# Attention plus feed-forward block: row exponentials of the first 128-row block gathered into one instruction, the sigmoid by exp and log, and small pieces evicted one unit later

## The chip, the cores and the metric

The kernel runs on one core of one Trainium2 chip. The metric is the device time of one execution in microseconds (us). A core has TensorE (PE; its weight loads are a row of their own, PEld), VectorE (DVE), ScalarE (ACT), GpSimd (POOL) and SyncE (SP, which here only issues DMAs). Each engine works through its own instructions in order and waits on semaphores for the others. Matmuls write to PSUM, eight banks of 128 partitions x 512 fp32; the other data lie in SBUF.

## The reference, cut to what matters

The input is 16 batches of 512 rows of 128 numbers. With `xn` the layer-normalised input, the output is `x + attention(xn) + ffn(xn)`:

```python
# attention: 16 heads, q and k of width 8, v of width 64, causal
scores = q @ k.T / sqrt(8); attn = softmax(scores masked above the diagonal); ctx = attn @ v; out = ctx @ Wo
# ffn: x_prev is xn one row earlier (zero at the first row)
xr = mu_r * xn + (1 - mu_r) * x_prev
xk = mu_k * xn + (1 - mu_k) * x_prev
r = sigmoid(xr @ W_r.T)
out = r * ((relu(xk @ W_k.T) ** 2) @ W_v.T)
```

## The kernel before, in words

All line numbers are those of the kernel before. A batch `b` is cut into 4 groups `g` of four heads (two pairs `w`, two heads `u` in each pair), and a group into 5 units `t`. So a batch has 20 units, and a unit number `n` runs through all batches (`n0 = 20 b`; in what follows "unit 14" is unit `n0 + 14`). `unit_work` (line 530) issues one unit. It does work for three places at once:

- For the group that is 11 units ahead, `rowscores` and `rowmask` (330, 343) compute on PE a 128-row block of scores for four heads, `sm`, two PSUM banks at a time with two buffers (`ps_sm`, 92); `rowmax` (357) takes the negated row maxima `negm` on DVE. `ROWS` (303) says which row blocks `i` a unit holds: kinds 0 and 2 a block of 384 columns (`i` = 2) and one of 128 (`i` = 0) for one pair; kinds 1 and 3 the 512 columns of `i` = 3; kind 4 the 256 columns of `i` = 1 for both pairs.
- For the group 10 units ahead (`LEAD`, 26), `rowsum` (376) does, for every block and head, one exp on ACT with the row's maximum as bias and the row sum as a second result (`accum_out`). After kind 4, `log_sums` (387) takes the logs; one unit later `sub_logs` and `turn_stats` (392, 396) turn `negm - log z` into rows by a PE transpose, `pm`, and `put_stats` (407) writes these, two units later, into extra rows of `q` by four DMAs on POOL's queue.
- For the unit itself, `scores` (422) computes the transposed scores `sT` (one buffer of two banks, `ps_st`, 93) with the softmax's normalisation already inside, `weights` (433) does one 128x1024 exp on ACT into `e` and zeroes the part above the diagonal on POOL, and `weigh` (445) multiplies by `v` into `av` (one bank, `ps_av`, 94), which `take_ctx` (460) copies out on DVE at the head of kinds 0 and 2.

Every other product goes through one PSUM bank, `m` (`ps_m`, line 95, one buffer): v (`project_v`, 245, eight per batch), q and k (`project_qk`, 218, each evicted twice, as a rounded high part `qh` and the remainder `ql`), the transposed input (`transpose_xn`, 207), the ffn products `ffn_r`, `ffn_k`, `ffn_out` (265, 284, 292), the output projection (`project_out`, 466, eight accumulating parts in two halves), and `pm`. I call these pieces.

The order is written out by hand. All engines keep the order in which the program issues instructions (`_InOrder`, 34). A table `at(n, piece)` (490 to 528) says in which unit a piece is issued; within a unit the order is: row scores, transposed scores, mask, `sub_logs`, `take_ctx`, `rowmax`, `rowsum`, `weights`, the pieces with their evictions, `weigh` (in kind 1 `weigh` comes ahead of the pieces), `turn_stats`. A piece's eviction is thus behind the unit's `rowmax` on DVE. Before, q is projected in unit 12, k in unit 17, v in units 1, 5, 10, 13, 14, 15, 16 and 18, the other ffn pieces in 0, 11 and 19, the transposes in 6, and the output projection of the batch before in 2, 2, 3, 4, 7, 7, 8, 9.

```python
def weights(b, g, t):
    e = ep.tile([P, 2, 512], FP, tag="e", name=f"e_{b}_{g}_{t}")
    act.activation(e, sts.pop((b, g, t)), AF.Exp)
...
def m_tile(name):
...
    return ps_m.tile([P, 512], FP, tag="m", name=name)
```

Of the kernel before, what the change touches and what calls it, by code (L numbers as in the profile page):

```python
# [27 lines left out]


FAR, NEAR = 2.0**43, 2.0**-84  # L30
SIG_MIN = -87.5


class _InOrder:
# [15 lines left out]
def attn_ffn_kernel(  # L50
# [156 lines left out]
    def transpose_xn(b):  # L207
        xn = xs.pop((b, "n"))
        pt = m_tile(f"xnTp_{b}")
        for c in range(NB):  # L210
            pe.transpose(pt[:, c * P : (c + 1) * P], xn[:, c, :], ident)

        xnT = big.tile([P, T + 1], FP, tag="xnT", name=f"xnT_{b}")
        pool.memset(xnT[:, 0:1], 0.0)
        dve.tensor_copy(xnT[:, 1 : T + 1], pt)
        xnTs[b] = xnT

    def project_qk(b, is_k, queue=sp):

        w, name = (wk, "k") if is_k else (wq, "q")  # L220
        pq = m_tile(f"p{name}_{b}")
        product(pq, w, xnTs[b][:, 1 : T + 1])
        hi = one.tile([P, T], FR, tag=f"{name}h", name=f"{name}h_{b}")
        lo = one.tile([P, T], FR, tag=f"{name}l", name=f"{name}l_{b}")
        dve.tensor_copy(hi, pq)
        dve.tensor_tensor(lo, pq, hi.bitcast(FP), ALU.subtract)

        blocks = (hi, lo, hi) if is_k else (hi, lo)
        d = dram.tile([len(blocks), P, T], FP, tag=name, name=f"{name}_{b}")
        for n, half in enumerate(blocks):  # L230
            queue.dma_start(out=d[n], in_=half.bitcast(FP))
        halves[b, name] = d.rearrange("n (d p u) t -> u (n d) p t", u=2, d=DK)
# [12 lines left out]
    def project_v(b, j, i):  # L245
        if j == 0 and i == 0:
            vs[b] = big.tile([P, NB, H * DV], FP, tag="v", name=f"v_{b}")
        pv = m_tile(f"pv_{b}_{j}_{i}")
        product(pv, xnTs[b][:, 1 + j * P : 1 + (j + 1) * P], wv[:, i * 512 : (i + 1) * 512])
        dve.tensor_copy(vs[b][:, j, i * 512 : (i + 1) * 512], pv)  # L250

    def mix_prev(b, i):
        prev = one.tile([P, T], FP, tag="prev", name=f"prev_{b}_{i}")
# [11 lines left out]
    def ffn_r(b):  # L265
        pr = m_tile(f"pr_{b}")
        product_turned(pr, xmix.pop((b, 0)), ffn_w[:, 0, :])
        e = one.tile([P, T], FP, tag="e_sig", name=f"e_sig_{b}")

        dve.tensor_scalar(e, pr, SIG_MIN, None, ALU.max)  # L270
        ffns[b, "e"] = e

    def ffn_exp(b):
        e = ffns[b, "e"]
        act.activation(e, e, AF.Exp, scale=-1.0)
        pool.tensor_scalar(e, e, 1.0, None, ALU.add)

    def ffn_sig(b, c):
        if c == 0:
            ffns[b] = one.tile([P, T], FP, tag="sig", name=f"sig_{b}")  # L280
        cols = slice(c * P, (c + 1) * P)
        dve.reciprocal(ffns[b][:, cols], ffns[b, "e"][:, cols])

    def ffn_k(b):
        pk = m_tile(f"pk_{b}")
        product(pk, ffn_w[:, 1, :], xmix.pop((b, 1)))
        kr = one.tile([P, T], FP, tag="kr", name=f"kr_{b}")
        dve.tensor_scalar(kr, pk, 0.0, None, ALU.max)
        pool.tensor_tensor(kr, kr, kr, ALU.mult)
        ffns[b, "k"] = kr  # L290

    def ffn_out(b):
        pk = m_tile(f"pkv_{b}")
        product_turned(pk, ffns.pop((b, "k")), ffn_w[:, 2, :])
        f = small.tile([P, T], FP, tag="ffn", name=f"ffn_{b}")
        dve.tensor_tensor(f, pk, ffns[b], ALU.mult)

        pool.tensor_tensor(f, f, xs.pop(b).rearrange("p c d -> p (c d)"), ALU.add)
        ffns[b] = f

# [22 lines left out]
        return (b, g, t) if 0 <= b < B else None  # L325


    stats, sms = {}, {}

    def rowscores(b, g, t):  # L330
        q, k = qs[b % 2], ks[b % 2]
# [25 lines left out]
    def rowmax(b, g, t):  # L357
# [11 lines left out]
            )  # L369
            return  # L370
        for w, i, to in blocks:
            dve.tensor_reduce(
                negm[:, :, w, i], sm[:, :, to : to + (i + 1) * P], AX.X, ALU.max, negate=True
            )

    def rowsum(b, g, t):
        negm, z = stats[b, g]
        sm = sms.pop((b, g, t))
        for w, i, to in ROWS[t]:
            for u in range(2):  # L380
                cols = sm[:, u, to : to + (i + 1) * P]
                act.activation(
                    cols, cols, AF.Exp,
                    bias=negm[:, u, w, i : i + 1], accum_out=z[:, u, w, i : i + 1],
                )

    def log_sums(b, g):
        lz = stat.tile([P, 2, 2, NB], FP, tag="lz", name=f"lz_{b}_{g}")
# [77 lines left out]
    def project_out(b, p):  # L466

        half = NPAIR // 2
        if p % half == 0:
            ffns[b, "po"] = m_tile(f"po_{b}_{p}")  # L470
        po = ffns[b, "po"]
        product_turned(
            po, ctxs.pop((b, p)), wo[:, p, :], start=(p % half == 0), stop=(p % half == half - 1)
        )
        if p == half - 1:
            y = one.tile([P, T], FP, tag="y", name=f"y_{b}")
            dve.tensor_tensor(y, po, ffns[b], ALU.add)
            ffns[b] = y
        elif p == NPAIR - 1:
            o = small.tile([P, NB, D], FP, tag="o", name=f"o_{b}")  # L480
            dve.tensor_tensor(o.rearrange("p c d -> p (c d)"), po, ffns.pop(b), ALU.add)
            sp.dma_start(out=out[b].rearrange("(c p) d -> p c d", p=P), in_=o)

    todo, subs, turns, puts = {}, {}, {}, {}

    def at(n, f, *args):  # L490
        todo.setdefault(n, []).append((f, args))

    per = UNITS * NPAIR // 2
    for b in range(B):
        n0 = b * per
        if b + 1 < B:
            r = 0 if b else 7
            at(n0 + r, ffn_r, b + 1)  # L500
            at(n0 + r + 1, ffn_exp, b + 1)
            for m, n in enumerate((1 if b else 3, 5, 10, 13, 14, 15, 16, 18)):
                at(n0 + n, project_v, b + 1, m // 2, m % 2)
            at(n0 + 6, mix_prev, b + 1, 1)
            at(n0 + 8, mix, b + 1, 1)
            at(n0 + 11, ffn_k, b + 1)
            at(n0 + 19, ffn_out, b + 1)
            for m, n in enumerate((-1, -1, 0, 0, 4, 4, 5, 5) if b else (0, 0, 0, 0, 4, 4, 5, 5)):
                at(n0 + n, spread_qk, b + 1, *SPREAD[m], slice(0, NPAIR // 2))
            for m, n in enumerate((8, 9, 9, 10, 10, 14, 14, 15)):  # L510
                at(n0 + n, spread_qk, b + 1, *SPREAD[m], slice(NPAIR // 2, NPAIR))
        if b + 2 < B:
            at(n0 + 4, deviation, b + 2)
            for c in range(NB):
                at(n0 + (1, 1, 3, 3)[c], row_moments, b + 2, c)
                at(n0 + 4 + c // 2, normalise, b + 2, c)
            at(n0 + 6, transpose_xn, b + 2)
            at(n0 + 12, project_qk, b + 2, False)
            at(n0 + 17, project_qk, b + 2, True)
            at(n0 + 11, mix_prev, b + 2, 0)  # L520
            at(n0 + 13, mix, b + 2, 0)
        for p, n in enumerate((2, 2, 3, 4, 7, 7, 8, 9) if b < B - 1 else (-8, -7, -7, -6, -3, -2, 0, 3)):
            at(n0 + per + n, project_out, b, p)
        if b + 1 < B:
            for c, n in enumerate((3, 7, 9, 14) if b else (11, 14, 17, 18)):
                at(n0 + n, ffn_sig, b + 1, c)
        if b + 3 < B:
            at(n0 + 11, load_x, b + 3)

    def unit_work(n):  # L530
# [10 lines left out]
        if n in subs:  # L541
            sub_logs(*subs.pop(n))
        t = n % UNITS
        done = {0: (n - UNITS, 0), 2: (n - UNITS, 1)}.get(t)
        if done and unit_of(done[0]):
            b, g, _ = unit_of(done[0])
            take_ctx(b, 2 * g + done[1])
        if stat_next:
            rowmax(*stat_next)

        if stat_now:
            rowsum(*stat_now)
            b, g, kind = stat_now
            if kind == UNITS - 1:
                log_sums(b, g)
                subs[n + 1] = turns[n + 1] = puts[n + 2] = b, g
        if now:
            weights(*now)
        pieces = todo.pop(n, ())
        if t != 1:  # L560
            for f, args in pieces:
                f(*args)
        since, w, blocks = WEIGHED[t]
        if unit_of(n - since):
            b, g, _ = unit_of(n - since)
            for j in blocks:
                weigh(b, 2 * g + w, j, (t, j) in ((1, 3), (4, 3)))
        if t == 1:
            for f, args in pieces:
                f(*args)  # L570
        if n in turns:
            turn_stats(*turns.pop(n))

    halves = {}

    qs, ks = [], []
# [18 lines left out]
    deviation(0)  # L595
    for c in range(NB):
        normalise(0, c, dve)
    transpose_xn(0)
    project_qk(0, False)
    project_qk(0, True, act)  # L600

# [36 lines left out]
    deviation(1)  # L640
    for c in range(NB):
        normalise(1, c, dve)
    transpose_xn(1)
    project_qk(1, False)
    first = -LEAD
    at(first + 1, project_qk, 1, True)
    for m, part in enumerate(SPREAD):
# [4 lines left out]
        at(first - 1 + 5 * i, mix_prev, 0, i)  # L652
        at(first + 1 + 6 * i, mix, 0, i)
    at(first + 8, ffn_r, 0)
    at(first + 9, ffn_exp, 0)
    for c, n in enumerate((1, 2, 3, 3)):
        at(n, ffn_sig, 0, c)
    at(2, ffn_k, 0)
    at(4, ffn_out, 0)
    at(1, mix_prev, 1, 0)  # L660
    at(5, mix, 1, 0)
    for n in range(first - 1, B * per + 2):
        if n == -1:
            lent.clear()
# [1 line left out]
    take_ctx(B - 1, NPAIR - 1)  # L666
    for n in sorted(todo):
        for f, args in todo[n]:
            f(*args)


# [29 lines left out]
```

## Time and profile before

| what | value |
|---|---|
| median of 3 runs | 1014.96 us (1014.45 to 1015.54) |
| the profiled execution, its own time | 1015.34 us |
| its span, first to last instruction | 1013.6 us |
| mean granted TensorE clock | 0.975 (1.00 in every stretch from 100 to 943 us) |
| logs `lz` of four successive groups, start | 508.03, 522.58, 537.12, 552.28; the next 567.36 us |
| one batch (20 units), from these | 59.33 us |
| first and last 128x1024 exp `e` (start) | 58.39 and 1002.38 us |

Nearly all instructions carry line 44, since a helper records them; they are told apart by their tiles. A group line gives out<-in by the program's names, the shapes, the count, then busy time in us and mean ns of one instruction, then the idle time of the engine just before and what ended it. A fp32 matmul appears as two records, so "x4" of `pv` is two products. A timeline line has start, length, engine, operation and, in brackets, idle time before it with its releaser. Instructions of one engine overlap at their ends, so I count a step from its start to the start of the next, not by its own length.

### The profile page before, as it was taken

What the parts mean: (1) busy time and instruction counts of PE and PEld (TensorE: products, weight loads), DVE (VectorE), ACT (ScalarE), POOL (GpSimd) and SP (SyncE); (2) the same over time, 40 slices, a digit from 0 to 9 for tenths busy, and PEclk for the clock granted to TensorE, in tenths of its full rate; (3) what the DMA queues carried; (4) which work ended last, traced back from release to release, by engine and by line L of the source; (5) the groups of instructions that cost most, each with busy time, mean ns of one, the idle gap of its engine ahead of it and who ended that gap; (6) DMA issues with size and microseconds to landing.
All of it is one profiled execution on the core that took longest, in us unless ns stands there. A gap on an engine that the chain in (4) does not pass through costs nothing.

```text
span 1013.6 us, 22825 instructions
## 1 busy us (share of the span) xinstructions
PE 949.4 (94%) x8131; PEld 524.4 (52%) x8131; DVE 790.4 (78%) x1312; ACT 921.6 (91%) x2449; POOL 512.4 (51%) x959
## 2 busy tenths in 40 slices
PE   3888999999999999999999999999999999999997
PEld 1244464555546455554645555464555646455454
DVE  4777878787887878788787878878787887877641
ACT  0688999999999999999999999999999999999982
POOL 4146364554646455454645555464465546434431
PEclk8578999999999999999999999999999999999999
DMA  8730513535142353514235341423534131343000
GB/s 183 134 45 13 110 19 70 91 70 91 34 101 28 70 91 70 90 34 99 31 70 90 70 91 34 96 34 70 90 71 81 33 95 25 70 80 49 3 13 11
DMA packets 59968, 67.10 MB, mean 66 GB/s; under 512 B 12928, under 2 KB 33024, under 8 KB 59856
## 3 DMA queue, kind: packets, MB, share of 16 engines
q1 hardware_dynamic: 48688, 61.89, 32.4%
q10 hardware_dynamic: 2528, 2.43, 1.0%
q0 software_dynamic: 8640, 1.34, 1.0%
q8 instruction: 65, 1.06, 0.5%
q14 instruction: 47, 0.39, 0.1%
HBM read 39.13 MB, written 25.17 MB: 63 GB/s over the span
## 4 chain that ended last, share of the span: by engine, by line
ACT 55%; PE 27%; issue 8%; DVE 7%; DMA 2%; POOL 1%; ACTq 0%; POOLq 0%
ACT sm L44 37%; ACT e L44 17%; PE av L44 9%; PE po L44 5%; DVE negm L44 4%; PE sm L44 4%; PE pv L44 3%; PE sT L44 3%; PE xnTp L44 1%; PE pr L44 1%; DVE xnT L44 1%; DMA q<-ml 1%; DVE v L44 1%; DMA k<-k 1%; PE pk L44 1%
## 5 line engine op out<-in xcount | busy, mean ns | idle before, releaser
L44 ACT ACTIVATE sm<-sm,negm 128x384 f32<-128x384 f32 (+3 forms) x1024 | 513.0, 501 | 64.9 <-DMA k<-k 27.3
L44 DVE TENSOR_REDUCE negm<-sm 128x2 f32<-128x768 f32 (+3 forms) x448 | 397.9, 912 | 101.3 <-PE sm L44 99.2
L44 POOL TENSOR_SCALAR_AFFINE_SELECT e<-e 128x256 f32<-128x256 f32 x512 | 200.5, 410 | 432.4 <-ACT e L44 432.3
L44 PE MATMUL av<-e,v 128*64 128x512 f32 (+3 forms) x2048 | 336.5, 438 | 2.4 <-DVE ctx L44 2.4
L44 ACT ACTIVATE e<-sT 128x1024 f32<-128x1024 f32 x320 | 324.1, 1013 | 14.1 <-PE sT L44 14.1
L44 PEld LDWEIGHTS av<-e,v 128*64 128x64 f32 x2048 | 139.7, 137 | 161.6 <-issue 129.6
L44 ACT ACTIVATION_READ_ACCUMULATOR sm<-sm,negm 128x1 f32 x1024 | 200.5, 196 | 0.0
L44 PE MATMUL sm<-k,q 33*128 33x384 f32 (+3 forms) x1024 | 164.8, 378 | 7.4 <-ACT sm L44 5.4
L44 PE MATMUL sT<-q,k 35*128 35x512 f32 (+3 forms) x1024 | 147.7, 335 | 16.5 <-ACT e L44 13.0
L44 PEld LDWEIGHTS sm<-k,q 33*128 33x128 f32 x1024 | 83.6, 188 | 151.8 <-ACT e L44 82.0
L44 PE MATMUL pv<-wv,xnT 128*64 128x512 f32 x512 | 142.3, 633 | 12.6 <-DVE kl L44 5.8
L44 PE MATMUL po<-wo,ctx 128*64 128x128 f32 x2048 | 133.2, 277 | 2.9 <-DVE ctx L44 1.6
L44 PEld LDWEIGHTS po<-wo,ctx 128*64 128x64 f32 x2048 | 109.8, 137 | 15.4 <-DVE v L44 2.6
L44 PEld LDWEIGHTS sT<-q,k 35*128 35x128 f32 x1024 | 91.2, 187 | 45.9 <-ACT e L44 40.0
L44 DVE COPY v<-pv 128x512 f32<-128x512 f32 x128 | 87.6, 684 | 23.2 <-PE pv L44 19.7
L44 DVE COPY ctx<-av 128x512 f32<-128x512 f32 x128 | 87.1, 680 | 12.7 <-PE av L44 12.6
L44 PE MATMUL sm<-mask,id 64*128 64x256 bf16 (+1 forms) x640 | 91.0, 265 | 0.0
L44 POOL DMA_DIRECT2D q<-mh x128 | 69.8, 548 | 24.9 <-DVE mh L44 12.8
L44 POOL DMA_DIRECT2D q<-ml x128 | 65.8, 519 | 0.0
L44 DVE RECIPROCAL sig<-e_sig 128x128 f32<-128x128 f32 x64 | 60.1, 940 | 0.0
L44 POOL TENSOR_SCALAR prev<-xnT,omm 128x512 f32<-128x512 f32 x32 | 50.0, 1564 | 16.2 <-DVE xmix L44 16.2
L44 PEld LDWEIGHTS <-id 64*128 64x128 bf16 x640 | 36.3, 95 | 24.8 <-issue 10.5
(63 smaller groups left out, 571.1 us busy)
## 6 DMA issues: line engine op xcount, KB each, us to landing
q<-q SPq DMA_DIRECT2D x124, 128.0 KB, 4.9
k<-k SPq DMA_DIRECT2D x124, 128.0 KB, 4.7
k<-kh SPq DMA_DIRECT2D x30, 256.0 KB, 2.6
x<-in_L_attn_x_dram SPq DMA_DIRECT2D x16, 256.0 KB, 6.5
q<-qh SPq DMA_DIRECT2D x16, 256.0 KB, 2.0
q<-ql SPq DMA_DIRECT2D x16, 256.0 KB, 2.1
out_dram<-o SPq DMA_DIRECT2D x16, 256.0 KB, 2.8
k<-kl SPq DMA_DIRECT2D x15, 256.0 KB, 2.0
```

The lines of the kernel that those rows point to most:

```text
L44: return self._tc.keep_in_program_order(f(*args, **kwargs))
```

## The change

It has three parts.

1. Row block `i` = 0 of a group's two pairs. `rowmax` now also adds `negm` to the 128-column block on DVE and writes it to a tile `first` in SBUF (one instruction in kind 0, one in kind 2, each 128 x 256). One exp on ACT over all 512 columns, `exp_first`, is issued in kind 2; one unit later DVE sums over it, `sum_first`. `rowsum` skips this block.
2. The sigmoid. Before: a lower limit on the way out of PSUM (DVE), an exp (ACT), +1 (POOL), and four reciprocals of 128x128 (DVE). After: a plain copy `r` out of PSUM (DVE), `low = min(r, 0)` and `r - 2 low` (POOL, one and two instructions), exp(-r) (ACT), log(1 + that) (ACT), `low - log` (POOL), exp (ACT). The three ACT steps are in units 10, 11 and 13, between the unit's row exps.
3. Where pieces stand. Most pieces now return their eviction as a function. A piece entered with `at_end` is issued on PE at the end of its unit, behind `weigh`, and its eviction at the head of the next unit: ahead of `take_ctx` and `rowmax` in kinds 1, 3 and 4, between the two in kind 2, behind `rowmax` in kind 0. v is in units 1, 2, 7, 12, 13, 16, 17, 18, the transposes in 11, `ffn_r` in 6, `ffn_k` in 14, `ffn_out` in 19, all by `at_end`. q is in unit 14 and k in unit 19, by plain `at` (issued ahead of `weigh`, evicted in the same unit). The output projection is in 3, 3, 4, 4, 8, 8, 9, 9. Layer norm and the mixes move by some units; two of the DMA sets that spread q and k over partitions swap places.

```diff
@@ rowmax / rowsum
+            if i == 0:
...
+                dve.tensor_tensor(
+                    firsts[b, g][:, w], cols, negm[:, :, w, 0:1].to_broadcast([P, 2, P]), ALU.add
+                )
...
+            if i == 0:
+                continue
...
+    def exp_first(b, g):
+        act.activation(firsts[b, g], firsts[b, g], AF.Exp)
+
+    def sum_first(b, g):
+        z = stats[b, g][1]
+        dve.tensor_reduce(
+            z[:, :, :, 0].rearrange("q u w -> q w u"), firsts.pop((b, g)), AX.X, ALU.add
+        )
@@ the table
-            for m, n in enumerate((1 if b else 3, 5, 10, 13, 14, 15, 16, 18)):
-                at(n0 + n, project_v, b + 1, m // 2, m % 2)
...
+            for m, n in enumerate((1, 2, 7, 12, 13, 16, 17, 18)):
+                at_end(n0 + n, project_v, b + 1, m // 2, m % 2)
...
+            at_end(n0 + 6, ffn_r, b + 1)
...
+            at_exps(n0 + 10, sig_exp, b + 1)
+            at_exps(n0 + 11, sig_log, b + 1)
+            at_exps(n0 + 13, sig, b + 1)
+            at_end(n0 + 14, ffn_k, b + 1)
+            at_end(n0 + 19, ffn_out, b + 1)
...
-            at(n0 + 12, project_qk, b + 2, False)
-            at(n0 + 17, project_qk, b + 2, True)
...
+            at_end(n0 + 11, transpose_xn, b + 2)
+            at(n0 + 14, project_qk, b + 2, False)
+            at(n0 + 19, project_qk, b + 2, True)
-        for p, n in enumerate((2, 2, 3, 4, 7, 7, 8, 9) if b < B - 1 else (-8, -7, -7, -6, -3, -2, 0, 3)):
+        for p, n in enumerate((3, 3, 4, 4, 8, 8, 9, 9) if b < B - 1 else (-8, -7, -7, -6, -3, -2, 0, 3)):
@@ unit_work
+        rest = pending.pop() if pending else lambda: None
+        if t % 2 or t == 4:
+            rest()
         done = {0: (n - UNITS, 0), 2: (n - UNITS, 1)}.get(t)
...
+        if t == 2:
+            rest()
         if stat_next:
             rowmax(*stat_next)
+        if t == 0:
+            rest()
...
-        pieces = todo.pop(n, ())
...
+        for f, args in todo.pop(n, ()):
+            rest = f(*args)
+            if callable(rest):
+                rest()
         since, w, blocks = WEIGHED[t]
...
+        if n in ends:
+            f, args = ends.pop(n)
+            pending.append(f(*args))
         if n in turns:
             turn_stats(*turns.pop(n))
```

## The prediction

> **What bounds the kernel now.** First the page's busy times, then the table of stretches for four successive groups (a group ends where its `lz` starts):
>
> ```profile
> PE 949.4 (94%) x8131; PEld 524.4 (52%) x8131; DVE 790.4 (78%) x1312; ACT 921.6 (91%) x2449; POOL 512.4 (51%) x959
> 508.03:522.58 14.55, 13.82 (x97) 6.39 (x95) 12.87 (x20) 14.16 (x39) 7.81 (x14) 1.00 0.47 105
> 522.58:537.12 14.54, 14.00 (x111) 7.09 (x109) 12.50 (x20) 14.15 (x39) 5.24 (x12) 1.00 0.33 92
> 537.12:552.28 15.16, 15.04 (x163) 9.71 (x161) 11.54 (x22) 14.74 (x39) 7.91 (x14) 1.00 0.62 79
> 552.28:567.36 15.08, 14.78 (x149) 9.24 (x147) 11.91 (x23) 14.33 (x39) 10.86 (x19) 1.00 0.01 2
> ```
>
> The columns are length, then PE, PEld, DVE, ACT and POOL busy. A batch takes 59.33 us. ACT runs gapless in the first two groups (14.55 us each: its instructions follow each other with 0.02 us between) and needs 0.52 more in the third for the sigmoid's exp: 4 x 14.55 + 0.5 = 58.7 us per batch. But PE is hardly less busy. Is that real work? PE's timeline of units 12 and 13 and, below it, DVE's answer:
>
> ```profile
> 515.01 0.50 PE L44 MATMUL sm<-k,q 33*128 33x512 f32 x2
> 515.35 0.40 PE L44 MATMUL sT<-q,k 35*128 35x384 f32 x4
> 515.59 0.23 PE L44 MATMUL sm<-mask,id 64*128 64x128 bf16 x2
> 515.88 1.08 PE L44 MATMUL pq<-xnT,wq 128*64 128x512 f32 x4
> 516.78 1.03 PE L44 MATMUL av<-e,v 128*64 128x512 f32 x4
> 517.74 0.50 PE L44 MATMUL sm<-k,q 33*128 33x256 f32 x4
> 518.08 0.39 PE L44 MATMUL sT<-q,k 35*128 35x512 f32 x2
> 518.32 0.28 PE L44 MATMUL sm<-mask,id 64*128 64x256 bf16 x2
> 519.02 0.65 PE L44 MATMUL pv<-wv,xnT 128*64 128x512 f32 x2 [0.41 <-DVE ql L44]
> ```
> ```profile
> 516.33 1.21 DVE L44 TENSOR_REDUCE negm<-sm 128x2 f32<-128x1024 f32 x1
> 517.47 0.68 DVE L44 CAST qh<-pq 128x512 fp32r<-128x512 f32 x1
> 518.18 0.69 DVE L44 TENSOR_TENSOR ql<-pq,qh 128x512 fp32r<-128x512 f32 x1
> ```
>
> Start to start, PE spends 0.34 + 0.24 + 0.29 us on scores and mask, 0.90 on q, 0.96 on `av`, and goes on at once. A full piece costs 0.91 us whatever stands next to it. Over the four groups PE stands still only before `sT` in the first unit of a group (0.42, 0.24, 0.23, 0.42 us, waiting for ACT's `e`) and twice before a `pv` that needs the bank that `ql` or `kl` still reads (0.48 each): 2.27 us. So **PE has 59.33 - 2.27 = 57.06 us of work per batch**, by group 13.8, 13.8, 14.7, 14.7. ACT is the bound by 1.7 us only.
>
> The Trainium skill (Perfetto Trace Analysis, Identifying the Most-Contended Engine) says that matmul busy time misjudges TensorE's headroom, and wants the share of weight loads instead. That share is 52%: by it PE would have room and the change could give what ACT loses, some 5 us per batch. The starts above say that it cannot give more than 2.3. I take the starts.
>
> **What the change takes from ACT.** ACT from the start of a kind 0 unit's last two exps:
>
> ```profile
> 545.61 0.34 ACT L44 ACTIVATE sm<-sm,negm 128x128 f32<-128x128 f32 x1
> 545.88 0.19 ACT L44 ACTIVATION_READ_ACCUMULATOR sm<-sm,negm 128x1 f32 x1
> 546.10 0.34 ACT L44 ACTIVATE sm<-sm,negm 128x128 f32<-128x128 f32 x1
> ```
>
> One 128-column exp with its sum costs 0.49 us from start to start. Four per group go: -1.96. One 128x512 exp comes; the nearest row is the sigmoid's exp, same shape from SBUF, 0.52 us from start to start: -1.44 per group, -5.76 per batch. The sigmoid has three such ACT steps for one: +1.04. ACT: 58.7 - 4.7 = **54.0 us**, no longer the bound.
>
> **DVE.** Two additions of 128x256 out of PSUM per group have no row; by the 128x256 reduce (0.415) and by half a 512 copy (0.34) I take 0.38. One 128x512 reduce from SBUF: by the copies, 0.62. So +1.4 per group, +5.5 per batch; four reciprocals of 0.85 go, -3.4. From 48.8 busy to 51 of about 60 us: not a bound in sum. Ends: if the addition cost its 0.68-us neighbours' price, 2.4 more per batch, still 53.
>
> **POOL.** The +1 (1.51) is replaced by `low` (about 1.5) and three subtractions (1.04 by `kr`, 1.27 by the `ffn` addition): +3.1 to +3.8 per batch on 32. Behind them stand the masks of `e`, used by `weigh` one or more units later; POOL waits 432 us in all for `e`, and that covers it. Without the cover a mask is late by one subtraction, 1.3 us, once or twice per batch. I take zero.
>
> **Queues.** q's two stores and k's three go to SP two units later, each with the spreads behind it. k's spreads stay in units 4 and 5 and are read in unit 9, four units (over 10 us) later; store and spread land in 2.6 and 4.7 us. Zero; if the order of the swapped q spreads cost a landing, 5 us per batch, which nothing speaks for.
>
> **Where the pieces go.** PE's work is the same, but what it waits for changes. The bank `m` has one buffer, so a piece cannot start before the last eviction of the piece before it.
>
> - *Unit 14*: q, `weigh`, then `ffn_k` at the end. On DVE q's two evictions stand behind `rowmax` of kind 0 and the new addition. From the unit's start on PE: reduce at 0.96 (so it stands in two such units of the four groups, 520.46 to 521.42 and 535.00 to 535.96), both reduces 1.31 (row: 1.29), addition 0.38, `qh` 0.71, `ql` 0.69, and 0.12 until PE's load: `ffn_k` can start at 4.17. PE has its scores (0.85), q (0.91) and `av` (0.96) behind it at 2.72. **PE stands 1.45 us.** *Unit 19* is the same with k and `ffn_out`: 1.45. In the kernel before the next piece came behind the next unit's scores, so only 0.48 was exposed.
> - *Units 0 and 15*: the eviction of `ffn_out` and `ffn_k` is behind `rowmax` (kind 0), and the transposition `pm` needs the bank. Reduce at 1.09 after the unit's start, 1.14, eviction 0.68, 0.14: `pm` at 3.05. PE has done scores (0.91) and `av` of 768 columns (1.32) at 2.23. **0.8 us each.** Before, a piece of 0.91 stood inside these units and filled the time; now nothing does.
> - In the other units the eviction at the head is in time: `v` is out 0.9 us after the unit begins, and its next user comes at 0.8 to 1.8. I put 0.3 per batch on the ones that just miss.
>
> The skill (same page, Optimizing Tensor Performance, Matmuls) asks that independent groups rotate through PSUM banks so that an eviction overlaps the next group's matmuls; with one bank the change puts two independent groups back to back. The `pv` row shows the price of that once, 0.48 us, with a whole score stage between; the page alone would give no number.
>
> The sum: waits of before gone, -2.27 (with ACT at 54 us `e` is early); waits new, 2 x 1.45 + 2 x 0.8 + 0.3 = +4.8. **A batch goes from 59.33 to 61.86 us, +2.5.** Low end, if PE gains on the units ahead and half of the `pm` waits vanish: +1.2. High end, if `sT` also waits in the group with the three sigmoid steps and DVE slips further (head evictions behind the sums): +3.9.
>
> **The whole run.** Batches 1 to 13 have everything: 13 x 2.5 = 32.5. Batch 14 has no q, k and transposes (57.06 - 2.7 + 1.9 = 56.3 against 59.3): -3.0. Batch 15 has no pieces but the output projection while its last row exps run; there ACT still bounds for two groups: -2 x 1.4 = -2.8. The ten units before the first `e` run ACT without PE's load, two groups: up to -2.9, I take -1.5 (the clock is lower and loads are waited for). Batch 0 lacks the output projections in its first half, where ACT gains what the second half loses: 0. The tail after the last row exps is PE's, unchanged. Sum +25. The profiled execution took 1015.3 us (span 1013.6, 1.7 outside it), 0.4 above the median: 1015.3 + 25 is about **1041 us**.
>
> **Rivals.**
> - *Faster: the new waits are hidden.* What would do it: DVE reaches q's evictions before `rowmax`'s input is there, or PE is late into units 14, 19, 0 and 15 because ACT held it just before, so that the waits fall into time lost anyway (unit 13 has a sigmoid step). Then PE has its 57.06 plus about 0.8: 57.9, -1.4 per batch, 13 x -1.4 - 7.3 = -26: 989 us. It decides from the point where the new waits together stay under 2.27 us. Against it: DVE's order has the reduces first, and each takes its 1.3 us only after PE's mask. Chance 0.13.
> - *Same*: new waits of 2.3 to 3.1 per batch (the start and end give 7 us back): 0.03.
> - *Slower than the forecast*: DVE becomes the pacer. The heads, the additions and the sums delay `rowmax` in kinds 0, 2 and 4, ACT's exps with it, and the `sm` buffers behind those; or POOL's subtractions delay a mask. A further 2 us per batch: 1068 us. For it: DVE at 51 busy of 62 with waits on both sides. Chance 0.09.
> - *The forecast*, 1024 to 1061: 0.75.
>
> Slower than before therefore 0.84, within 0.2% (what a measurement of this kernel can tell from no change) 0.03, faster 0.13. The range 1017 to 1064 takes in the forecast's ends and a part of the cases beside them.
>
> **What would show it.** In the profile after: PE's loads of `pk` and `pkv` waiting for DVE `ql` and `kl` about 1.4 us in some 14 cases each; `pm` waiting for DVE `kr` and `ffn` about 0.8 us; ACT busy near 850 us with gaps in front of `sm` and `e`; groups of 14.9 to 16.3 us, the longest with k and `ffn_out`; DVE near 825 us. It is wrong if units 14 and 19 last under 4 us on PE, or if ACT is still gapless.

## The result

The changed kernel takes **1057.14 us** (median of 4 runs, 1055.31 to 1057.5) against 1014.71 us for the kernel before in the same comparison: ratio 1.042, 95% interval 1.0395 to 1.0446. It is slower, as forecast; 1041 was predicted and the range went to 1064. The profiled execution has a span of 1055.1 us, 41.5 more than before. One execution of the kernel with part 2 alone (below) took 1707.98 us, against 1038.56 to 1039.58 for its other three; it was in a slower state and is in no number here, and its trace, the only one of that kernel, is not read.

Busy times first, then the stretches of four successive groups of one batch (columns as above: length, PE, PEld, DVE, ACT, POOL busy, and then the granted TensorE clock, 1.00 as before):

```profile
PE 942.5 (89%) x8131; PEld 514.9 (49%) x8131; DVE 844.1 (80%) x1440; ACT 864.5 (82%) x2033; POOL 573.1 (54%) x1007
```
```profile
451.03:466.02 14.99, 14.41 (x159) 9.36 (x157) 12.62 (x25) 13.27 (x32) 11.45 (x18) 1.00 0.01 2
466.02:481.46 15.44, 14.76 (x127) 7.89 (x121) 13.36 (x22) 14.27 (x35) 10.48 (x18) 1.00 0.31 53
481.46:497.29 15.83, 13.72 (x97) 5.99 (x95) 13.25 (x22) 13.15 (x32) 6.16 (x13) 1.00 0.15 51
497.29:513.13 15.84, 14.10 (x143) 8.35 (x141) 13.16 (x24) 13.15 (x31) 7.94 (x14) 1.00 0.87 153
```

ACT lost 57 us of work, PE has the same work, and still the span grew: no engine is busy throughout any more. In the last two groups PE works 13.7 and 14.1 us out of 15.8. The chain of work that ended last, as shares of the span by engine, has moved from ACT to PE and DVE (before, then after):

```profile
ACT 55%; PE 27%; issue 8%; DVE 7%; DMA 2%; POOL 1%; ACTq 0%; POOLq 0%
PE 56%; DVE 22%; ACT 9%; issue 8%; POOL 2%; DMA 2%; ACTq 0%; DVEq 0%; POOLq 0%
```

What PE waits for stands in unit 14 (PE's timeline; the numbers at the end are idle time and releaser):

```profile
543.28 1.08 PE L43 MATMUL pq<-xnT,wq 128*64 128x512 f32 x4
544.19 1.03 PE L43 MATMUL av<-e,v 128*64 128x384 f32 x8
546.62 1.08 PE L43 MATMUL pk<-xmix,ffn_w 128*64 128x512 f32 x4 [1.39 <-DVE ql L43]
547.62 0.50 PE L43 MATMUL sm<-k,q 33*128 33x512 f32 x2
547.97 0.40 PE L43 MATMUL sT<-q,k 35*128 35x512 f32 x2
548.21 0.23 PE L43 MATMUL sm<-mask,id 64*128 64x128 bf16 x2
548.37 1.51 PE L43 MATMUL av<-e,v 128*64 128x512 f32 x8
550.45 0.27 PE L43 MATMUL pm<-ident,lz 128*16 128x128 f32 x1 [0.57 <-DVE kr L43]
```

`ffn_k` (`pk`) stands 1.39 us because `ql` still reads the bank, and in the next unit `pm` stands 0.57 because `kr` does. The chain goes this way there (start, length, what; lines left out are marked):

```profile
543.39 1.30 DVE negm L43 x2
...
545.06 0.69 DVE qh L43
...
545.78 0.70 DVE ql L43
...
546.62 1.08 PE pk L43 x4
...
549.62 0.69 DVE kr L43
```

From each unit's first `sm` matmul on PE to the next unit's, median over batches 2 to 13, in us (worked out from PE's timelines; the column "rearranged" belongs to an experiment below):

| unit | before | after | rearranged | | unit | before | after | rearranged |
|---|---|---|---|---|---|---|---|---|
| 0 | 3.66 | 3.02 | 3.88 | | 10 | 3.84 | 2.61 | 2.84 |
| 1 | 2.72 | 2.72 | 2.72 | | 11 | 2.72 | 2.44 | 2.44 |
| 2 | 3.62 | 2.61 | 2.61 | | 12 | 2.73 | 2.87 | 2.88 |
| 3 | 2.25 | 3.19 | 3.19 | | 13 | 2.72 | 2.23 | 2.23 |
| 4 | 2.73 | 3.60 | 3.61 | | 14 | 2.71 | **5.64** | 2.97 |
| 5 | 3.84 | 2.60 | 2.60 | | 15 | 3.66 | 3.02 | 3.88 |
| 6 | 2.64 | 2.73 | 2.74 | | 16 | 2.72 | 2.71 | 2.71 |
| 7 | 3.61 | 3.11 | 2.61 | | 17 | 2.73 | 2.61 | 2.61 |
| 8 | 2.25 | 3.18 | 3.19 | | 18 | 2.72 | 2.23 | 2.23 |
| 9 | 2.73 | 3.61 | 3.61 | | 19 | 2.73 | **5.27** | 2.97 |
| | | | | | sum | 59.33 | **62.01** | 58.51 |

A batch is 62.0 us; 61.86 was forecast. The rest of the 41.5 us lies at the ends. Measured between the same `e` exps in both traces, against the forecast's terms:

| stretch | forecast | measured |
|---|---|---|
| up to the first `e` | -1.5 | -1.4 |
| batch 0 | 0 | **+4.8** |
| batches 1 to 13 | +32.5 | +36.8 |
| batch 14 | -3.0 | **-0.2** |
| first half of batch 15 | -2.8 | **+0.9** |
| the rest | 0 | +0.5 |

In batch 0, GpSimd's `low` waits for the eviction of batch 0's `ffn_out`, which reads the only buffer of the tile `low` in unit 8 (POOL's timeline, then ACT's):

```profile
86.99 1.52 POOL L43 TENSOR_SCALAR low<-r 128x512 f32<-128x512 f32 x1 [3.38 <-DVE ffn L43]
88.52 1.58 POOL L43 TENSOR_SCALAR xn<-x,mv,rstd 128x128 f32<-128x128 f32 x2
90.06 0.40 POOL L43 TENSOR_SCALAR_AFFINE_SELECT e<-e 128x256 f32<-128x256 f32 x1
90.44 2.60 POOL L43 TENSOR_TENSOR r<-r,low 128x512 f32<-128x512 f32 x2
```
```profile
89.24 0.56 ACT L43 ACTIVATE sm<-sm,negm 128x384 f32<-128x384 f32 x1
93.08 0.63 ACT L43 ACTIVATE r<-r 128x512 f32<-128x512 f32 x1 [3.17 <-POOL r L43]
```

The sigmoid's step stands between two row exps on ACT, so the row exps, and all that needs them, wait 3.17 us with it. In one later batch (the one from 500 us; the wait ends at 532.46) this step waits 2.28 us for GpSimd and the batch takes 63.5 instead of 62.0; why GpSimd is late there was not followed.

### The profile page after: what moved, and what is told of

It reads as the page before. It is cut to its first block, busy times and chain, and to the rows that moved or that the text cites. A ratio compares the mean times of both kernels' runs of the same rounds, so it can differ in the third digit from the quotient of the medians.

```text
span 1055.1 us, 22666 instructions
## 1 busy us (share of the span) xinstructions
PE 942.5 (89%) x8131; PEld 514.9 (49%) x8131; DVE 844.1 (80%) x1440; ACT 864.5 (82%) x2033; POOL 573.1 (54%) x1007
## 4 chain that ended last, share of the span: by engine, by line
PE 56%; DVE 22%; ACT 9%; issue 8%; POOL 2%; DMA 2%; ACTq 0%; DVEq 0%; POOLq 0%
PE av L43 16%; PE po L43 11%; PE sm L43 11%; DVE negm L43 8%; PE pv L43 6%; PE sT L43 6%; ACT sm L43 4%; ACT e L43 3%; DVE ctx L43 3%; PE pk L43 2%; PE pkv L43 1%; DVE first L43 1%; PE pm L43 1%; DVE z L43 1%; DVE v L43 1%
## 5 line engine op out<-in xcount | busy, mean ns | idle before, releaser
L43 ACT ACTIVATE sm<-sm,negm 128x384 f32<-128x384 f32 (+2 forms) x768 | 425.8, 554 | 114.6 <-DVE first L43 31.1
L43 PE MATMUL av<-e,v 128*64 128x512 f32 (+3 forms) x2048 | 346.3, 448 | 17.2 <-DVE ctx L43 14.0
L43 PEld LDWEIGHTS av<-e,v 128*64 128x64 f32 x2048 | 129.5, 137 | 139.3 <-issue 105.7
L43 ACT ACTIVATION_READ_ACCUMULATOR sm<-sm,negm 128x1 f32 x768 | 151.7, 198 | 0.0
L43 PE MATMUL sT<-q,k 35*128 35x512 f32 (+3 forms) x1024 | 139.9, 330 | 9.5 <-ACT e L43 7.2
L43 PE MATMUL pv<-wv,xnT 128*64 128x512 f32 x512 | 137.0, 611 | 0.6 <-DVE r L43 0.6
L43 PE MATMUL po<-wo,ctx 128*64 128x128 f32 x2048 | 126.6, 276 | 1.7 <-DVE ctx L43 1.6
L43 DVE COPY ctx<-av 128x512 f32<-128x512 f32 x128 | 87.3, 682 | 14.1 <-PE av L43 12.8
L43 POOL DMA_DIRECT2D q<-mh x128 | 70.1, 551 | 38.9 <-DVE mh L43 32.5
L43 PE MATMUL sm<-mask,id 64*128 64x256 bf16 (+1 forms) x640 | 87.0, 264 | 0.0
L43 DVE TENSOR_TENSOR first<-sm,negm 128x256 f32<-128x256 f32 x128 | 54.4, 425 | 4.4
L43 PEld LDWEIGHTS pv<-wv,xnT 128*64 128x64 f32 x512 | 36.2, 139 | 41.1 <-issue 18.1
```

The lines of the kernel that those rows point to most:

```text
L43: return self._tc.keep_in_program_order(f(*args, **kwargs))
```

## The experiments

Theory: PE is the bound after the change, and the loss is its waits for the one bank `m`, made by the new places of the pieces (part 3). Rival: VectorE, with the additions and sums of part 1, or GpSimd and ScalarE with the sigmoid of part 2, make the loss. All ratios are to the kernel before, run on the same chip, with 95% intervals.

### Each part alone

**Part 1 alone.** The kernel before with the additions, `exp_first`, `sum_first`, and the skipped exps; nothing else of the diff above.

> The kernel before with part 1 alone (row block 0: VectorE addition and sum, one exp); its schedule and its sigmoid stay. Bank theory (TensorE is the bound, and the loss of the change comes from its waits for the one bank m): ScalarE falls to about 53 us per batch, TensorE keeps its 57.1 of work, loses its waits for e and keeps the two of 0.48: 58.2 per batch instead of 59.3, total 995 to 1006 us. Rival (the additions and sums make VectorE the pacer): slower than 1020 us.

Measured: 1033.73 us, ratio 1.0205 (1.0178 to 1.0232). My theory missed and the rival's 1020 was exceeded. A batch takes 60.87 us; against the kernel before, units 5, 10 and 15 grow (3.84 to 4.35, 3.84 to 4.17, 3.66 to 4.63), all of kind 0. On DVE there is no gap from 514.96 us on, through units 8 to 10:

```profile
514.96 1.23 DVE L44 TENSOR_REDUCE negm<-sm 128x4 f32<-128x1024 f32 x1 [1.13 <-PE sm L44]
516.11 0.90 DVE L44 SCALAR_TENSOR_TENSOR xmix<-xnT,mus,prev 128x512 f32<-128x512 f32 x1
516.92 0.67 DVE L44 TENSOR_REDUCE z<-first 128x4 f32<-128x512 f32 x1
517.52 1.27 DVE L44 TENSOR_REDUCE negm<-sm 128x2 f32<-128x768 f32 x2
518.83 0.43 DVE L44 TENSOR_TENSOR first<-sm,negm 128x256 f32<-128x256 f32 x1
519.17 0.68 DVE L44 TENSOR_TENSOR o<-po,y 128x512 f32<-128x512 f32 x1
519.77 0.94 DVE L44 RECIPROCAL sig<-e_sig 128x128 f32<-128x128 f32 x1
520.63 0.11 DVE L44 TENSOR_TENSOR lz<-negm,lz 128x16 f32<-128x16 f32 x1
520.66 0.68 DVE L44 COPY ctx<-av 128x512 f32<-128x512 f32 x1
521.25 1.22 DVE L44 TENSOR_REDUCE negm<-sm 128x2 f32<-128x1024 f32 x1
```

The sum (0.60) and the addition (0.34) are put into a stretch that already held a mix, an eviction and a reciprocal; PE's mask for the last reduce was done at 520.44, 0.8 us before it could start. PE meets this through the two evictions beside that reduce:

```profile
520.37 1.08 PE L44 MATMUL pv<-wv,xnT 128*64 128x512 f32 x4
521.48 1.51 PE L44 MATMUL av<-e,v 128*64 128x512 f32 x8
523.12 0.28 PE L44 MATMUL pm<-ident,lz 128*16 128x128 f32 x1
```

`av` starts when `ctx` is out (520.66 + 0.68 = 521.34), and `pm` when `v` has left the bank `m` (522.38 + 0.68 = 523.06). The wait for ACT's `e` did not grow: from a unit's first `sm` to its `sT` PE takes 0.75 us in units 5 and 10, as before, and 0.43 in unit 15 instead of 0.58. So the rival holds here, locally: VectorE has room in sum, but not in this stretch, and its delay reaches PE through the PSUM banks that it empties.

**Part 2 alone.** The kernel before with the sigmoid's new steps: `ffn_r` in unit 0, `low` in 1, the subtractions in 2, ACT's steps in 4, 5 and 7.

> The kernel before with part 2 alone (sigmoid by exp, log and exp with GpSimd's steps, instead of exp and reciprocals). ScalarE, the bound there, gets two more steps of 0.52 us per batch: +1.0 x 15, so 1028 to 1034 us by the bank theory. By the rival that GpSimd's steps delay the masks or that ScalarE waits for them: above 1040 us.

Measured: 1039.12 us (median of three), ratio 1.0264 (1.0242 to 1.0286), 5 us or more beyond what the two ACT steps explain. The run without part 3, below, has the sigmoid's steps in the same places and shows a cause that would fit; that it acts here was not shown.

**Part 3 alone.** The changed kernel with parts 1 and 2 undone; ACT's exp in unit 10, the reciprocals put by me in units 11, 12, 16 and 17.

> The changed kernel with parts 1 and 2 undone: only the places of the pieces and of their evictions are new; the four reciprocals are put in units 11, 12, 16 and 17, the exp in unit 10. Bank theory: the waits in units 14 and 19 are 1.1 each without the addition, those of pm 0.7 each: TensorE 57.1 + 3.6 to 4.2, 60.7 to 61.3 per batch, total 1035 to 1045 us. Rival (parts 1 and 2 make the loss): 1010 to 1022 us.

Measured: 1037.24 us, ratio 1.024 (1.0213 to 1.0267): within the forecast of the bank theory. Units 14 and 19 take 4.73 and 4.74 us, against 5.64 and 5.27 with all parts; a batch takes 60.84. PE waits there 0.91 us each before `pk` and `pkv` and 0.57 before each `pm`, 3.0 per batch for the one bank. Not all of the 25 us come from the new places: in units 12 and 17 one of my reciprocals stands ahead of `ctx` on DVE, and `av` waits 0.55 and 0.27 us for it, some 12 us over 15 batches.

### One part undone

**Without part 2.** The changed kernel with the exp in unit 10 and the reciprocals put by me in units 11, 12, 16 and 17.

> The changed kernel with part 2 undone (exp in unit 10, reciprocals in units 11, 12, 16 and 17): parts 1 and 3 stay. Bank theory: the four waits for the bank stay, but ScalarE loses its two steps and never waits for GpSimd, so that sT is early in units 11, 12 and 14 (about 0.9 us per batch), and batch 0 loses its wait of about 4 us: 1038 to 1046 us. If the sigmoid is the main cause: below 1025 us.

Measured: 1069.97 us, ratio 1.0565 (1.0543 to 1.0588), slower than with part 2; both theories missed. The unit times show that it is the places I gave the reciprocals: units 12 and 17 take 3.68 and 3.41 instead of 2.87 and 2.61, 1.6 us per batch, since a reciprocal of 0.85 us, behind the addition, stands ahead of `ctx` there and `av` waits 1.00 and 0.72 us. The run therefore says little about the sigmoid beyond the start, where batch 0 takes 65.2 instead of 71.5 us.

**Without part 1.** The changed kernel; `rowsum` does block 0 again.

> The changed kernel with part 1 undone: parts 2 and 3 stay. ScalarE is back at 59.8 us per batch and TensorE's waits in units 14 and 19 are shorter by the addition, 0.35 each. Bank theory: about 61.5 to 62.5 per batch, 1048 to 1060 us, so next to the changed kernel. Rival (the additions and sums pace): 1030 us or less.

Measured: 1057.54 us, ratio 1.0462 (1.0438 to 1.0485), as the bank theory has it: 62.26 per batch. Units 14 and 19 fall to 5.22 and 4.85 (the addition is gone from the chain), but units 10, 11 and 13 grow by 0.3 to 0.55 each, where ACT carries the sigmoid's steps on top of the old exps. Part 1 neither makes nor heals the loss as long as the bank waits are there.

**Without part 3.** The old places with parts 1 and 2.

> The changed kernel with part 3 undone: the pieces stand and are evicted as in the kernel before, with parts 1 and 2. Bank theory: 58.2 to 58.7 per batch, 998 to 1012 us, faster than the kernel before. Rival (parts 1 and 2 make the loss): above 1030 us.

Measured: 1038.1 us, ratio 1.0256 (1.0234 to 1.0277). A miss for me again: 60.98 per batch. One unit stands out, unit 6 with 3.90 instead of 2.64 us. PE there:

```profile
570.11 0.44 PE L43 MATMUL xnTp<-ident,xn 128*128 128x128 f32 x2
571.10 0.33 PE L43 MATMUL xnTp<-ident,xn 128*128 128x128 f32 x1 [0.55 <-POOL xn L43]
571.88 0.33 PE L43 MATMUL xnTp<-ident,xn 128*128 128x128 f32 x1 [0.45 <-POOL xn L43]
```

The transposes wait for the normalised input, which GpSimd makes only after the sigmoid's subtractions. That is a cost of POOL's, which I had put at zero (for the new places).

**The same, with the sigmoid's steps later**: `low` and the subtractions in units 7 and 8, ACT's steps in 10, 15 and 17.

> Parts 1 and 2 on the old schedule, as in the run without part 3, but GpSimd's sigmoid steps go from units 1 and 2 to 7 and 8, and ScalarE's to 10, 15 and 17. In that run the transposes of unit 6 waited for the normalised input, which stood behind the sigmoid's subtractions on GpSimd (unit 6 took 3.90 instead of 2.64 us). If that is so: unit 6 back at 2.65, 59.3 to 59.7 us per batch, 1011 to 1022 us. If the additions and sums alone make the loss, as in the run of part 1 alone: 60.9 per batch, 1034 us.

Measured: 1018.36 us, ratio 1.0049 (1.0027 to 1.007). Unit 6 is back at 2.64 and a batch at 59.91: the move gains some 20 us, and 1.26 per batch of it are the transposes' wait for GpSimd. What stays against the kernel before is 0.6 us per batch, in units 0 and 15 (4.03 and 3.83 instead of 3.66). It also bears on part 1 alone: the additions and sums stand here as there, but the reciprocals are gone from VectorE, and units 5, 10 and 15 take 3.87, 3.84 and 3.83 instead of 4.35, 4.17 and 4.63.

### The disputed waits

**The bank waits removed.** In the changed kernel:

```diff
-            at_end(n0 + 14, ffn_k, b + 1)
-            at_end(n0 + 19, ffn_out, b + 1)
+            at(n0 + 15, ffn_k, b + 1)
+            at(n0 + 20, ffn_out, b + 1)
```

> The changed kernel, with only ffn_k moved from the end of unit 14 into unit 15 and ffn_out from the end of unit 19 into the unit after, ahead of weigh, so that q and k are evicted before the bank is wanted and the piece stands where pm waited. Bank theory: units 14 and 19 shrink by 2.2 to 2.6 us, the next units grow by 0.4: -4 to -4.4 per batch, 57.6 to 58 per batch, total 995 to 1010 us. Rival (VectorE paces): units 14 and 19 lose only the piece's own 0.9 and the next gain it: above 1040 us.

Measured: 1019.86 us, ratio 1.0074 (1.0053 to 1.0094), above the 995 to 1010 that I expected and far below the rival's 1040: some 35 of the 42 us are gone by moving two pieces by one unit. Units 14 and 19 take 3.17 and 3.01, units 15 and 0 take 4.07 and 3.84. The gain per batch is 2.8, not the 4 to 4.4 of my expectation, because the next units grew by 0.8 to 1.05 and not by 0.4: `sT` now waits in them for ACT's `e`, 0.48 us in unit 15 and 0.24 in unit 0. This is the run that decides for the bank theory: parts 1 and 2 are untouched in it.

**The start.** `ffn_out` of batch 0 in unit 4 instead of 8, nothing else.

> The changed kernel with one number changed: ffn_out of batch 0 in unit 4 instead of unit 8. In the changed kernel the next batch's min(r, 0) waits there for this product's eviction, because the tile low has one buffer, and ScalarE's sigmoid step, ahead of its row exps, waits 3.2 us for GpSimd. If that wait is what lengthened batch 0 (71.5 us against 66.8 before): batch 0 falls by 3 to 4.5 us and the total to 1051 to 1054 us, about 0.35% less. If batch 0 is long for another reason: no change.

Measured: 1050.29 us, ratio 1.0364 (1.0339 to 1.0388), against 1.042 for the changed kernel: batch 0 takes 64.3 instead of 71.5 us. The gain is some 6 to 7 us, more than the 3.17 us that ACT waited and more than I expected. The move also takes the product out of unit 8; what each of the two is worth was not separated.

**The bank waits removed, without part 2.** The kernel of the run without part 2, with the same two lines moved as above.

> The changed kernel with the sigmoid as before and with ffn_k and ffn_out in units 15 and 20, ahead of weigh. Bank theory: TensorE near its 57.1 of work per batch, 57.2 to 57.8, total 985 to 998 us; the best of all versions so far. Rival: no faster than part 1 alone.

Measured: 1038.02 us, ratio 1.025 (1.0214 to 1.0286), 60.7 per batch. The move again gains some 32 us, but units 12 and 17 (3.68 and 3.41) still carry my reciprocals, which the 985 to 998 us that I expected left out. A miss, and not all of it is explained: without the 1.9 us that the reciprocals add in these two units a batch would still be 58.8, where I expected 57.2 to 57.8.

**All three parts rearranged.**

```diff
-            for m, n in enumerate((1, 2, 7, 12, 13, 16, 17, 18)):
+            for m, n in enumerate((1, 2, 7, 12, 14, 16, 17, 19)):
                 at_end(n0 + n, project_v, b + 1, m // 2, m % 2)
...
-            at_exps(n0 + 11, sig_log, b + 1)
-            at_exps(n0 + 13, sig, b + 1)
-            at_end(n0 + 14, ffn_k, b + 1)
-            at_end(n0 + 19, ffn_out, b + 1)
+            at_exps(n0 + 15, sig_log, b + 1)
+            at_exps(n0 + 20, sig, b + 1)
+            at(n0 + 15, ffn_k, b + 1)
+            at(n0 + 20, ffn_out, b + 1)
...
-            at(n0 + 6, deviation, b + 2)
+            at(n0 + 5, deviation, b + 2)
...
-            at(n0 + 14, project_qk, b + 2, False)
-            at(n0 + 19, project_qk, b + 2, True)
+            at_end(n0 + 13, project_qk, b + 2, False)
+            at_end(n0 + 18, project_qk, b + 2, True)
...
-    at(8, ffn_out, 0)
+    at(4, ffn_out, 0)
```

The head's evictions also come ahead of `sub_logs` and `rowmax` in kind 0 units.

> All three parts, with the pieces placed so that no two that share the bank stand back to back without an eviction between: q and k at the end of units 13 and 18, v at the end of 14 and 19, ffn_k and ffn_out ahead of weigh in 15 and 20; evictions of kind 0 units at the head too; the last two sigmoid steps in units 15 and 20; the layer norm's deviation in unit 5; ffn_out of batch 0 in unit 4. Bank theory: TensorE's waits fall under 1 us per batch, 57.4 to 58.2, total 988 to 1004 us, faster than both kernels. Rival (VectorE cannot keep up with the additions and sums): 59 or more per batch, 1015 us or more.

Measured: **998.51 us, ratio 0.9852 (0.9831 to 0.9873)**: faster than both kernels, and within the forecast of the total; a batch is 58.51, 0.3 above its 58.2. Four groups of one batch:

```profile
582.53:596.93 14.40, 14.10 (x140) 8.41 (x139) 13.07 (x25) 13.32 (x33) 7.93 (x14) 1.00 0.86 143
596.93:611.65 14.72, 14.58 (x163) 9.53 (x161) 12.81 (x25) 13.14 (x31) 11.25 (x18) 1.00 0.01 3
611.65:626.63 14.98, 14.40 (x122) 7.65 (x117) 13.17 (x21) 13.44 (x33) 9.11 (x17) 1.00 0.36 71
626.63:641.02 14.39, 14.10 (x98) 6.35 (x95) 13.08 (x22) 13.31 (x32) 7.44 (x14) 1.00 0.26 66
```

DVE and ACT do what they did in the changed kernel (52.1 and 53.2 us per batch against 52.4 and 53.8); only PE's waits went, 62.0 to 58.5 (its named waits in batches 2 to 13 are 59.0 us in the changed kernel and 14.5 here). PE in unit 14, where q is evicted while the scores run and v takes the bank at the end:

```profile
624.04 0.50 PE L43 MATMUL sm<-k,q 33*128 33x384 f32 x4
624.40 0.50 PE L43 MATMUL sT<-q,k 35*128 35x384 f32 x4
624.74 0.28 PE L43 MATMUL sm<-mask,id 64*128 64x256 bf16 x2
624.96 1.08 PE L43 MATMUL av<-e,v 128*64 128x384 f32 x8
626.00 1.08 PE L43 MATMUL pv<-wv,xnT 128*64 128x512 f32 x4
```

**The rearranged kernel without part 1.**

> The rearranged kernel (all three parts, q and k at the end of units 13 and 18 and so on) with part 1 undone: what is part 1 worth once the bank's waits are gone? ScalarE is back at about 58.8 + 1.0 = 59.8 us per batch, gapless, above TensorE's 57.1: 59.8 to 60.5 per batch, total 1012 to 1025 us, so part 1 is worth 1.3 to 2 us per batch. If part 1 cost as much on VectorE as it saves on ScalarE: 58.0 to 58.8 per batch, about 998 us, as with it.

Measured: 1026.41 us, ratio 1.0121 (1.0093 to 1.0148), 60.29 per batch, as forecast (the total is 1.4 us above it), against 58.51 with part 1. By busy time PE is ahead:

```profile
PE 955.0 (93%) x8131; PEld 521.3 (51%) x8131; DVE 769.2 (75%) x1248; ACT 932.4 (91%) x2481; POOL 574.8 (56%) x1007
```

But ACT is the bound again: in batches 2 to 13 PE's `sT` waits 18.0 us for ACT's `e`, against 7.3 with part 1, while ACT waits only for GpSimd's `r`, 8.7 us. Part 1 is worth some 27 us once the places fit; in the changed kernel it was worth nothing that shows.

## Why the prediction was right, and where it was not

- *PE has 57.06 us of work and ACT bounds by 1.7 us only.* Right. In the rearranged kernel a batch takes 58.5 us with ACT at 53 us, so it is PE's work with 1.4 us of waits. The gain that the weight loads' share of 52% would have allowed (the Trainium skill, Perfetto Trace Analysis, Identifying the Most-Contended Engine, names it together with MFU, the share of peak arithmetic, which was not worked out) is not there in any run: the share is 49% in the changed kernel and 52% in the fastest.
- *ACT loses 4.7 us per batch.* From start to start the exchange is as costed: a kind 2 unit's row exps took 2.25 us (544.21 to 546.46 in the trace before) and take 1.65 with the new exp in between (520.53 to 522.18 after). ACT's busy time fell by 57.1 us only, to 864.5 and not 850, because an instruction whose successor waits is counted to its end: the lengths of all ACT instructions, added up, fell by 74 us, from 1062.7 to 988.4. VectorE's busy time came out at 844 and not 825; that was not followed.
- *Units 14 and 19 wait 1.45 us each for the bank.* Right: 1.39 in the fence above, 1.4 and 1.2 in most batches (19.2 us in 14 cases behind `ql`, 16.3 in 14 behind what follows `kl`). Unit 14 was longer than the sum by 0.5, of which 0.40 is `sT` waiting for an `e` that the sigmoid's last step in unit 13 made late (without part 2 this wait is gone); that stood in the forecast's high end only.
- *Units 0 and 15 wait 0.8 us each for `pm`.* Too large: 0.57 and 0.57. The reduce ahead of the eviction starts 0.86 us after the unit's start (548.48, for 547.62) and not 1.09.
- *The other units 0.3.* Too small. `av` waits for `ctx` in four units, 0.44 us in unit 7, 0.20 in unit 12 and 0.15 each in 5 and 10. In units 7 and 12 part 1's addition stands ahead of `ctx` on DVE, in unit 7 `deviation` too (without part 1 the rearranged kernel has 2.6 us in both units, instead of 3.11 and 2.87).
- *The sum.* PE's named waits in batches 2 to 13 come to 4.9 us per batch, against 4.8: before `pk` and `pkv` 2.6 (forecast 2.9), before `pm` 1.1 (1.6), all others 1.2 (0.3). The two large terms were right in kind and too big, the small one too small by 0.9, and these errors cancel: that 61.86 comes so near to 62.0 is in part luck.
- *The ends.* This is the term that was mis-sized, and it accounts for most of the 16 us between 1041 and 1057: forecast -7.3 (start, batch 0, batches 14 and 15), measured +4.6; the other 4.3 are in batches 1 to 13. For batch 0 I looked at PE and ACT and not at the new tile `low`, which has one buffer and is read by a piece that the same change had moved from unit 4 to unit 8; the run with that piece in unit 4 gives 7 us back. For batch 14 I put 54.4 us of PE's work and 1.9 of waits against 59.3 before. By the traces PE is busy for 55.5 and idle for 3.1 us there (0.57 and 0.56 before `pm`, 0.24 and 0.49 before `sT`, 0.43 before `av`), and before the batch had taken 58.8. In the first half of batch 15 I took ACT to be gapless. It waits twice there for VectorE's new addition, 0.89 and 0.78 us, and PE's `av` waits 0.78 us twice for the `ctx` that stands behind this addition. For these batches I had counted the addition as VectorE's time only.
- *POOL at zero.* Right for the steady state of the changed kernel, but for the one batch with the 2.28 us, and wrong in general: on the old schedule the same subtractions delay the transposes by 1.25 us in every batch.
- *Queues at zero.* Right: in batches 2 to 13 no wait of PE ends with a DMA.
- *The rival "VectorE paces".* It was given 0.09. In the changed kernel as a whole it isn't what bounds, since moving two pieces gives some 35 us back with VectorE's work unchanged. But it is real locally, and part 1 on the old schedule is slower for it. I had costed VectorE by its sum over a batch.

## What to carry to other kernels

When two engines are within 3% of each other, taking work from one is worth at most that difference, and the price of a new order shows in the other: write out, unit by unit, when each single-buffered tile is free again on the engine that evicts it. A load that fits in the sum over a period may still not fit in the stretch where it is put; look for the longest gapless stretch of the engine that gets the work, and for the PSUM banks that it empties at the end of it. If a change that saves work makes a kernel slower, find the waits and move the pieces before undoing it: here the same three parts are 4.2% slower or 1.5% faster.

## What the runs showed of the hardware

VectorE instructions with two inputs from SBUF were held up by GpSimd. In the changed kernel the subtraction `lz` (128x16, median 0.195 us) took 0.94 us once, under GpSimd's subtractions (POOL, then DVE):

```profile
529.81 2.62 POOL L43 TENSOR_TENSOR r<-r,low 128x512 f32<-128x512 f32 x2
```
```profile
530.18 0.94 DVE L43 TENSOR_TENSOR lz<-negm,lz 128x16 f32<-128x16 f32 x1
```

It ended with the first of the two. It is no single case. In the traces of all these kernels but that of part 2 alone, `lz` started 58 times while one of these subtractions had 0.2 us or more to go; it then took 0.34 to 0.94 us and each time ended 0.03 to 0.04 us after GpSimd's instruction. With no GpSimd instruction beside it (236 cases) it never took over 0.18. The addition `first`, with one input from PSUM and one from SBUF, took 0.42 to 0.43 us in 72 such cases, as it does alone. The Trainium skill (SBUF — State Buffer, SBUF: two separate sides) says that a VectorE instruction with two SBUF inputs and a GpSimd one that reads SBUF exclude each other for a whole instruction, and these rows fit. So do most of GpSimd's masks of `e` (217 of 229 cases). Beside GpSimd's TENSOR_SCALAR instructions (`xn`, `prev`, the sigmoid's +1), which read SBUF too, the rule does not show: in all 31 such cases `lz` ended before GpSimd's instruction did, after 0.16 to 0.53 us. There the measurement decides. The mix `xmix`, also with two inputs from SBUF, took 0.99 us in 14 of 28 cases of the steady stretch, at most 0.85 before.

ACT's exps over 384 columns waited for VectorE's addition over the other 128 columns of the same tile (31.1 us in 62 cases named `first`; where the profile names `pv` the exp also starts 0.10 us after the addition's end, 553.35 to 553.45). In the steady stretch ACT had the time, so this cost nothing that shows; in batch 15 it is part of the loss above.
